# A Perceiver block on one core: filler steps as lists with kinds and lags, VectorE's parts held back, gating by tanh on ScalarE and GpSimd

## The chip, the core and the metric

The kernel runs on one core of a Trainium2 chip. The core's engines each work through their own queue in order: TensorE (PE; its weight loads are the row PEld), VectorE (DVE), ScalarE (ACT), GpSimd (POOL) and SyncE (SP, which here only issues transfers). The metric is the device time of one execution in microseconds; three executions of the kernel before gave 1245.61, 1246.41 and 1250.19 us.

## The reference

64 sequences of 64 rows of 256 numbers (`x`) pass through three residual stages; `ctx_1024` holds 256 context rows for each sequence. There are 16 heads of 16 numbers, everywhere in fp32.

```python
x = x + _L0_xattn_ref(_layernorm(x), ctx_1024, ctx_1024, Wq, bq, Wk, bk, Wv, bv, Wo, bo)   # 64 queries, 256 keys
x = x + _L0_attn_ref(_layernorm(x), w_qkv, b_qkv, w_out, b_out)                            # causal, 64 keys
x = x + _L0_ffn_ref(_layernorm(x), w_gate, w_up, w_down)
...
gate = jax.nn.silu(_bitlinear(x, w_gate)); up = _bitlinear(x, w_up)
return _bitlinear(gate * up, w_down)          # inner width 1024
```

`_bitlinear` quantises each row of its input to steps of its largest magnitude over 127 and the weights to -1, 0 and 1 times one scale. Silu is `silu(z) = z * sigmoid(z)`, which equals `(z/2) * (1 + tanh(z/2))`.

## The kernel before

The 64 sequences ("images") form 8 groups of 8. The main loop (L659 to L700) runs over images, and each image does its cross attention; the self attention of the group before and the feed-forward of the group before that are cut into steps that fill the gaps. The order of instructions on PE, ACT, DVE and POOL is the order in which the program issues them (`manual_schedule`, L645): nothing reorders them later. An instruction whose input is late therefore holds everything behind it on its engine.

Cross attention of image n, in the order of issue:

- `scores` (L260): TensorE writes all 16 heads' scores transposed into one PSUM tile `sc` of four banks. There is one such tile (`bufs=1`), so the next image's scores wait until this one's Exp has read it. VectorE then reduces it with a transposition to maxima `tm` (L275) and `m` (L279).
- `cross_av` (L318) of the image before: TensorE multiplies its probabilities `PT` by the values into `av`, and sums of them `PS` by ones; ScalarE takes one half of the rows (`keep`, L335).
- `project` (L632): one of four quarters of the next image pair's keys (L219, L232) or values (L239, L242).
- `fill()`: filler steps.
- `cross_keep` (L339) takes the other half of the rows on VectorE.
- `max_rows` (L284): TensorE transposes the maxima (`mtp`, L288), and a chain of six VectorE instructions (L290 to L297) turns them into bf16 rows `mr`.
- `cross_out` (L341): VectorE's reciprocal (L342) and multiplication (L344) give `yT_a`.
- `probabilities` (L301): TensorE subtracts the maxima by adding products of `mr` (L306); ScalarE takes Exp of `sc` into `PT` in two halves (L313); GpSimd adds the two key halves into `PS` (L315).
- `project` and `fill` again, and the next image's `scores`.

In an image there are five calls of one filler step each: one ahead of `max_rows`, one ahead of `probabilities`, one after it, two ahead of the next `scores`. The steps are two Python generators, `self_attention` (L347) and `ffn` (L497), and `fill` (L593) takes one step from each in turn until one is exhausted. What is left at the start of a group is run out by `drain` (L601). A list `later` takes a few VectorE parts (L433, L535) and is emptied ahead of the next step; other VectorE parts are issued inside their steps: the masking, maxima and sums of the self attention (L387, L390, L401), the residual additions (L252, L562), layer-norm statistics (L177), the row scales of the quantisation (L488 to L494). `prepare` (L609) does the next group's layer norm and queries, one part per image from image 1 of a group on, after the load of its `x` (L83).

The self attention works on 128-row tiles: scores `ssc` (L381), masking and maxima on VectorE, subtraction on GpSimd (L391), Exp on ScalarE (L395), sums on VectorE (L401), division on GpSimd (L403), transposition (L411), product `sav` (L426), output projection (L249).

The feed-forward takes its four row tiles one after the other. `gate_up` (L525) computes one half of the inner width: two products gate and up of 512 columns in PSUM (L529), Silu of gate on ScalarE into SBUF (L532), and on VectorE `up * unit * silu` into `h` (L538). Two calls make a row tile. Then come the row scale (L488 to L494), two roundings on ScalarE (L544, L548), transposition (L553, L555), the down product (L560) and the addition to `x` (L562); `out[g]` is stored from GpSimd's queue (L580).

Every product that is not `sc` uses one of four PSUM tiles `mm` (L69), taken in turn. After the last image, group 7's self attention runs with group 6's feed-forward, and then group 7's feed-forward alone.

Of the kernel before, what the change touches and what calls it, by code (L numbers as in the profile page):

```python
# [34 lines left out]
P = 128  # L36
D = 256
# [21 lines left out]
def tile_perceiver(ctx: ExitStack, tc: tile.TileContext, a: dict, out: bass.AP):  # L59
# [137 lines left out]
    def ln_apply(src, y, b, name):  # L197

        xn = act.tile([P, NI, D], F32, tag="xn", name=f"xn_{name}", bufs=3)
        for i in range(NI):  # L200
            nc.scalar.activation(xn[:, i, :], src[:, i, :], AF.Identity, bias=b[:, i:i + 1],
                                 scale=y[:, i:i + 1])
        return xn
# [40 lines left out]
    def add_projected(w, yT, xg, name, i0):  # L244

        pm = mm_tile(f"o_{name}_{i0}")
        for i in range(2):
            for kc in range(KC):
                nc.tensor.matmul(pm[:, i * D:(i + 1) * D],  # L249
                                 yT[:, kc, (i0 + i) * P:(i0 + i + 1) * P], w[:, kc, :],  # L250
                                 start=(kc == 0), stop=(kc == KC - 1))
        nc.vector.tensor_tensor(xg[:, i0:i0 + 2, :], pm.rearrange("p (i d) -> p i d", d=D),  # L252
                                xg[:, i0:i0 + 2, :], ALU.add)
# [30 lines left out]
    def max_rows(n, m3):  # L284
# [5 lines left out]
        nc.vector.tensor_reduce(x, pt[:, 0:P].rearrange("p (r i) -> p i r", i=32), AX.X, ALU.max,  # L290
                                negate=True)
        for k in range(2):
            t = small.tile([P, 32], BF16, tag="mt", name=f"mt_{n}_{k}")
            nc.vector.tensor_copy(t, x)
            nc.vector.scalar_tensor_tensor(x, t, term[:, k:k + 1], x, ALU.mult, ALU.add)
# [22 lines left out]
    def cross_av(n, pT, pS, v):  # L318
# [17 lines left out]
        return a4, t  # L336

    def cross_keep(a4, t):
        nc.vector.scalar_tensor_tensor(t, a4[:, :, 1, :], par[:, 1:2], t, ALU.mult, ALU.add)  # L339

    def cross_out(n, t, yT):  # L341
        nc.vector.reciprocal(t[:, KC:, :], t[:, KC:, :])  # L342
        b = n % G
        nc.vector.tensor_tensor(yT[:, :, b * T:(b + 1) * T], t[:, 0:KC, :], t[:, KC:, :], ALU.mult)  # L344


    def self_attention(g, xg, yTa):  # L347
        nm = f"s{g}"
        mv = moments(nm)
        for i0 in range(0, NI, 2):  # L350
            add_projected(wT["o"], yTa, xg, f"a{g}", i0)
            ln_stats(xg, nm, mv, (i0, i0 + 1))
            yield
        y, shift = ln_rstd(mv, nm)
        yield
        xn = ln_apply(xg, y, shift, nm)
        yield
        xnT = act.tile([P, KC, NT], F32, tag="xnT", name=f"xnT_{nm}")
        for kc in range(KC):
            transposed(xn, nm, xnT, kc)  # L360
        yield
        qm = act.tile([P, KC, G, 2, T], F32, tag="sqm", name=f"sqm_{g}", bufs=1)
        kT = act.tile([P, KC, NT], F32, tag="skT", name=f"skT_{g}", bufs=1)
        v = act.tile([P, NI, D], F32, tag="sv", name=f"sv_{g}", bufs=1)
        for hg in range(KC):
            queries(wqkv, bqm2, xnT, nm, qm, hg)
            yield
            keys(wqkv, D, bqkc[:, KC + hg:KC + hg + 1], xnT, nm, kT, hg)
            yield
        yT = act.tile([P, KC, NT], F32, tag="yT", name=f"yT_{nm}", bufs=3)  # L370
        s, pTs = {}, {}

        def scores(hg, j0):
# [3 lines left out]
            for b in range(G):  # L377
                for h in range(2):
                    for i in range(2):
                        r = slice(2 * E * (j0 + i), 2 * E * (j0 + i + 1))  # L380
                        nc.tensor.matmul(scs[i][h * T:(h + 1) * T, b * T:(b + 1) * T],  # L381
                                         qm[r, hg, b, h, :], kT[r, hg, b * T:(b + 1) * T],
                                         start=True, stop=True)
            for i in range(2):
                k = f"{nm}_{hg}_{j0 + i}"
                t = s[hg, j0 + i] = att.tile([P, G, T], F32, tag="s", name=f"s_{k}", bufs=4)
                nc.vector.tensor_tensor(t, scs[i].rearrange("p (b k) -> p b k", k=T),  # L387
                                        causal.unsqueeze(1).to_broadcast([P, G, T]), ALU.add)
                mx = small.tile([P, G], F32, tag="smax", name=f"smax_{k}")
                nc.vector.tensor_reduce(mx, t, AX.X, ALU.max)  # L390
                nc.gpsimd.tensor_tensor(t, t, mx.unsqueeze(2).to_broadcast([P, G, T]), ALU.subtract)  # L391
# [5 lines left out]
        def normalise(hg, j0):  # L397
            for j in (j0, j0 + 1):
                t = s[hg, j]
                tot = small.tile([P, G], F32, tag="stot", name=f"stot_{nm}_{hg}_{j}")  # L400
                nc.vector.reduce_sum(tot, t, axis=AX.X)  # L401
                nc.vector.reciprocal(tot, tot)  # L402
                nc.gpsimd.tensor_tensor(t, t, tot.unsqueeze(2).to_broadcast([P, G, T]), ALU.mult)  # L403
# [14 lines left out]
        def product(hg):  # L418

            av = [mm_tile(f"sav_{g}_{hg}_{bl}") for bl in range(2)]  # L420
            for bp in range(G // 2):
                for bl in range(2):
                    r = slice(bl * T, (bl + 1) * T)
                    for j in range(NJ):
                        d0 = hg * P + 2 * E * j
                        nc.tensor.matmul(av[bl][2 * E * j:2 * E * (j + 1), bp * P:(bp + 1) * P],  # L426
                                         v[r, bp, d0:d0 + 2 * E], pTs[hg, j][r, bp, :], start=True,
                                         stop=True)
            for bl in range(2):
# [3 lines left out]
                later.append(lambda bl=bl, a4=a4, t=t: keep(hg, bl, a4, t))  # L433

        def keep(hg, bl, a4, t):
            y4 = yT[:, hg, :].rearrange("p (bp bl q) -> p bp bl q", bl=2, q=T)
# [3 lines left out]
        scores(0, 0)  # L440
        yield
        values(wqkv, 2 * D, xnT, nm, v, 0)
        exps(0, 0)
        yield
        scores(0, 2)
        normalise(0, 0)
        yield
        values(wqkv, 2 * D, xnT, nm, v, 2)
        exps(0, 2)
        yield  # L450
        transpose(0, 0)
        normalise(0, 2)
        yield
        scores(1, 0)
        yield
        transpose(0, 2)
        exps(1, 0)
        yield
        scores(1, 2)
        normalise(1, 0)  # L460
        yield
        product(0)
        exps(1, 2)
        yield
        transpose(1, 0)
        normalise(1, 2)
        yield
        add_bias(xg, bo2_r, 0)
        yield
        transpose(1, 2)  # L470
        yield
        product(1)
        add_bias(xg, bo2_r, 2)
        yield
        mv = mvs[g] = moments(f"f{g}")
        for i0 in range(0, NI, 2):
            add_projected(wout, yT, xg, nm, i0)
            ln_stats(xg, f"f{g}", mv, (i0, i0 + 1))
            yield
# [17 lines left out]
    def ffn(g, xg):  # L497
        nm = f"f{g}"
        mv = mvs.pop(g)
        y, shift = ln_rstd(mv, nm)  # L500
        yield
        xn = ln_apply(xg, y, shift, nm)
        yield
        scale, unit = row_scale(xn, f"x{g}")
        u = small.tile([P, 2, NI], F32, tag="units", name=f"units_{g}", bufs=2)
        nc.vector.tensor_scalar(u[:, 0, :], unit, g_unit, None, ALU.mult)
        nc.vector.tensor_scalar(u[:, 1, :], unit, u_unit, None, ALU.mult)
        yield
        for i in range(NI):
            nc.vector.tensor_scalar(xn[:, i, :], xn[:, i, :], scale[:, i:i + 1], MAGIC, ALU.mult,  # L510
                                    ALU.add)
        q = act.tile([P, NI, D], BF16, tag="q", name=f"q_{nm}", bufs=1)
        nc.scalar.activation(q, xn, AF.Identity, bias=unmagic)
        yield
        pt = mm_tile(f"qtp_{nm}", BF16)
        for i in range(NI):
# [260 lines left out]
```

## Time and profile before

| what | us |
|---|---|
| median of the runs | 1246.41 |
| the profiled execution | 1248.42 |
| its span, first to last instruction | 1246.7 |
| DVE L275, maxima with transposition, each | 2.302 |
| ACT L313, Exp of half of `sc`, each | 1.020 |
| POOL L315, `PS`, each | 1.270 |
| POOL L391, subtraction, each | 1.043 |
| DVE L538, gating, each | 0.747 |
| ACT L532, Silu, each | 0.687 |
| ACT table loads ahead of L532, L313, L395 and L201: 27, 18, 8, 1, each | 1.283 |
| TensorE waiting at L306 for `mr`, in all | 110.3 |
| GpSimd waiting at L315 for `PT`, in all | 390.7 |

How to read it: a group row gives line, engine, operation, output and inputs with their shapes, the number of instances, then their busy time and mean duration in ns, then the idle time of the engine ahead of them with what ended it. The row of a window gives its length and the busy time of PE, PEld, DVE, ACT and POOL (with counts), the granted TensorE clock, the share of the DMA engines and GB/s. A timeline row gives start, duration, engine, line and instruction, and in brackets the engine's idle time before it and what ended it.

### The profile page before, as it was taken

What the parts mean: (1) busy time and instruction counts of PE and PEld (TensorE: products, weight loads), DVE (VectorE), ACT (ScalarE), POOL (GpSimd) and SP (SyncE); (2) the same over time, 40 slices, a digit from 0 to 9 for tenths busy, and PEclk for the clock granted to TensorE, in tenths of its full rate; (3) what the DMA queues carried; (4) which work ended last, traced back from release to release, by engine and by line L of the source; (5) the groups of instructions that cost most, each with busy time, mean ns of one, the idle gap of its engine ahead of it and who ended that gap; (6) DMA issues with size and microseconds to landing.
All of it is one profiled execution on the core that took longest, in us unless ns stands there. A gap on an engine that the chain in (4) does not pass through costs nothing. (4 is left out here: it accounts for less than half of the span.)

```text
span 1246.7 us, 25915 instructions
## 1 busy us (share of the span) xinstructions
PE 955.5 (77%) x11086; PEld 630.8 (51%) x11086; DVE 778.2 (62%) x1616; ACT 665.8 (53%) x934; POOL 412.2 (33%) x502
## 2 busy tenths in 40 slices
PE   6666688887787788787787787788886887676755
PEld 3444456564455545564455554555454654553532
DVE  1465667656667756576666765767575766775634
ACT  2233255436764386536774377544864467536635
POOL 1234335332235323334143422443134422341330
PEclk9878898988998898888998998988988888888868
DMA  6111000000001000010000100010000100000000
GB/s 197 52 51 52 18 18 19 18 19 17 18 19 36 18 34 1 19 52 18 18 18 2 52 18 18 18 52 18 18 2 18 35 18 1 2 18 1 1 18 17
DMA packets 10195, 32.44 MB, mean 26 GB/s; under 512 B 2400, under 2 KB 2784, under 8 KB 9696
## 3 DMA queue, kind: packets, MB, share of 16 engines
q1 hardware_dynamic: 7056, 26.22, 6.4%
q0 software_dynamic: 1152, 4.19, 0.8%
q8 instruction: 87, 1.43, 0.5%
q10 hardware_dynamic: 1872, 0.37, 0.2%
q14 instruction: 28, 0.23, 0.1%
HBM read 26.59 MB, written 4.19 MB: 25 GB/s over the span
## 5 line engine op out<-in xcount | busy, mean ns | idle before, releaser
L315 POOL TENSOR_TENSOR PS<-PT 128x512 f32<-128x512 f32 x128 | 159.9, 1270 | 390.7 <-ACT PT L313 390.7
L275 DVE TRANSPOSE_TENSOR_REDUCE tm<-sc 128x64 f32<-128x2048 f32 x64 | 147.3, 2302 | 96.1 <-PE sc L271 96.0
L313 ACT ACTIVATE PT<-sc 128x1024 f32<-128x1024 f32 x128 | 123.9, 1020 | 123.4 <-PE sc L306 123.2
L219 PE MATMUL k_a<-cT,wk 128*128 128x512 f32 x256 | 144.3, 694 | 6.8 <-DMA wk<-in_wk_dram 5.6
L239 PE MATMUL v_a<-wv,cT 128*128 128x256 f32 x512 | 144.6, 432 | 1.2 <-ACT sqm L227 1.2
L391 POOL TENSOR_TENSOR s_s<-s_s,smax_s 128x512 f32<-128x512 f32 x64 | 66.7, 1043 | 226.5 <-DVE smax_s L390 221.3
L538 DVE SCALAR_TENSOR_TENSOR h_f<-up_f,units,silu_f 128x512 f32<-128x512 f32 x64 | 47.8, 747 | 125.0 <-ACT silu_f L532 124.1
L239 PEld LDWEIGHTS v_a<-wv,cT 128*128 128x128 f32 x512 | 104.8, 214 | 32.7 <-issue 12.6
L306 PE MATMUL sc<-mr,ones 32*128 32x512 bf16 x256 | 31.1, 470 | 110.8 <-DVE mr L297 110.3
L335 ACT ACTIVATE keep<-av,par 128x256 f32<-128x256 f32 x64 | 30.3, 473 | 134.0 <-PE av L331 134.0
L219 PEld LDWEIGHTS k_a<-cT,wk 128*128 128x128 f32 x256 | 54.0, 223 | 60.5 <-issue 50.9
L232 ACT ACTIVATE kT<-k_a,bk_c 128x512 f32<-128x512 f32 x64 | 43.9, 688 | 72.2 <-PE k_a L219 72.1
L271 PE MATMUL sc<-qm,kT 32*128 32x128 f32 x2048 | 79.0, 292 | 1.5 <-ACT qm L227 0.9
L271 PEld LDWEIGHTS sc<-qm,kT 32*128 32x128 f32 x2048 | 66.3, 195 | 24.6 <-issue 14.0
L306 PEld LDWEIGHTS <-ones 32*128 32x128 bf16 x256 | 11.3, 93 | 132.8 <-issue 130.8
L326 PE MATMUL av<-PT,v 128*32 128x128 f32 x2048 | 74.7, 289 | 0.0
L387 DVE TENSOR_TENSOR s_s<-ssc,causal 128x512 f32<-128x512 f32 x64 | 43.9, 685 | 48.0 <-PE ssc L381 48.0
L403 POOL TENSOR_TENSOR s_s<-s_s,stot_s 128x512 f32<-128x512 f32 x64 | 65.4, 1043 | 5.7 <-DVE stot_s L402 3.0
L342 DVE RECIPROCAL keep<-keep 128x128 f32<-128x128 f32 x64 | 60.5, 945 | 0.0
L326 PEld LDWEIGHTS av<-PT,v 128*32 128x32 f32 x2048 | 55.6, 115 | 9.1 <-issue 1.2
L529 PEld LDWEIGHTS <-qT_f 128*128 128x128 bf16 x256 | 25.8, 104 | 63.3 <-issue 47.4
L560 PE MATMUL down_f<-wq_down,hqT_f 128*128 128x256 bf16 x256 | 41.8, 319 | 20.0 <-ACT hqT_f L555 20.0
(159 smaller groups left out, 1970.5 us busy)
## 6 DMA issues: line engine op xcount, KB each, us to landing
cT<-in_ctx_dram SPq DMA_DIRECT2D x32, 512.0 KB, 3.6
x<-in_x_dram SPq DMA_DIRECT2D x8, 512.0 KB, 3.6
out_dram<-x POOLq DMA_DIRECT2D x8, 512.0 KB, 3.2
wffn_gate<-in_wgate_dram SPq DMA_DIRECT2D x1, 1024.0 KB, 4.8
wffn_up<-in_wup_dram SPq DMA_DIRECT2D x1, 1024.0 KB, 4.9
wffn_down<-in_wdown_dram SPq DMA_DIRECT2D x1, 1024.0 KB, 4.8
wqkv<-in_wqkv_dram SPq DMA_DIRECT2D x1, 768.0 KB, 6.2
wk<-in_wk_dram SPq DMA_DIRECT2D x1, 256.0 KB, 4.3
```

Source lines behind the costliest of these rows:

```text
L219: nc.tensor.matmul(pm, w[:, kc, c0:c0 + P], src[:, kc, :], start=(kc == 0), stop=(kc == KC - 1))
L232: nc.scalar.activation(kT[:, hg, :], pm, AF.Identity, bias=bias)
L239: nc.tensor.matmul(pm[:, i * D:(i + 1) * D], src[:, kc, (i0 + i) * P:(i0 + i + 1) * P], w[:, kc, c0:c0 + D], start=(kc == 0), stop=(kc == ...
L271: nc.tensor.matmul(sc[:, j, c, hg, :], kT[r, hg, k0 + c * P:k0 + (c + 1) * P], qm[r, hg, b, :, :].rearrange("p h q -> p (h q)"), start=not ...
L275: nc.vector.tensor_reduce(tm.rearrange("p j c m -> p (j c m)"), sc.rearrange("p j c g (b i) -> p (j c g b) i", i=32), AX.X, ALU.max, apply ...
L313: nc.scalar.activation(pT[:, j:j + 2].rearrange("p j c g q -> p j (c g q)"), sc[:, j:j + 2].rearrange("p j c g q -> p j (c g q)"), AF.Exp)
L315: nc.gpsimd.tensor_tensor(pS[:, j:j + 2], pT[:, j:j + 2, 0], pT[:, j:j + 2, 1], ALU.add)
L326: nc.tensor.matmul(av[2 * E * j:2 * E * (j + 1), hg * P:(hg + 1) * P], v[:, (n % 2) * SC + c, d0:d0 + 2 * E], pT[:, j, c, hg, :], start=(c ...
L342: nc.vector.reciprocal(t[:, KC:, :], t[:, KC:, :])
L391: nc.gpsimd.tensor_tensor(t, t, mx.unsqueeze(2).to_broadcast([P, G, T]), ALU.subtract)
L403: nc.gpsimd.tensor_tensor(t, t, tot.unsqueeze(2).to_broadcast([P, G, T]), ALU.mult)
L538: nc.vector.scalar_tensor_tensor(h[i][:, 0, n0:n0 + 512], up, u[:, 1, i:i + 1], sl, ALU.mult, ALU.mult)
```

## The change

Every filler becomes a list of steps `(kind, lag, function)`. Kind "H" marks steps whose VectorE parts are long, "L" steps that ScalarE finishes, and "Z" steps that issue nothing on TensorE; a lag is the least number of places until the step may run. Almost all VectorE parts of steps go into `later` with a length in microseconds, and so does the cross attention's output part (`cross_out` now holds `cross_keep` too). `fill(kind)` runs at most one step per place beside "Z" steps, with preference for a kind. Of a feed-forward's list the last four steps stay behind (`LEFT`) for the next group's first images. Output projections are split into one step per row tile. The store follows the last step of its list, `x` is loaded and `prepare` begun one image later, and `xn` has two buffers instead of three.

```diff
-        nc.vector.tensor_reduce(x, pt[:, 0:P].rearrange("p (r i) -> p i r", i=32), AX.X, ALU.max,
-                                negate=True)
         for k in range(2):
             t = small.tile([P, 32], BF16, tag="mt", name=f"mt_{n}_{k}")
-            nc.vector.tensor_copy(t, x)
+            if not k:
+                for o in (x, t):
+                    nc.vector.tensor_reduce(o, pt[:, 0:P].rearrange("p (r i) -> p i r", i=32), AX.X,
+                                            ALU.max, negate=True)
+            else:
+                nc.vector.tensor_copy(t, x)
...
+        later.append((1.4, lambda: cross_out(n, a4, t, yT)))
+    def cross_out(n, a4, t, yT):
         nc.vector.scalar_tensor_tensor(t, a4[:, :, 1, :], par[:, 1:2], t, ALU.mult, ALU.add)
         nc.vector.reciprocal(t[:, KC:, :], t[:, KC:, :])
-        nc.vector.tensor_tensor(yT[:, :, b * T:(b + 1) * T], t[:, 0:KC, :], t[:, KC:, :], ALU.mult)
+        nc.gpsimd.tensor_tensor(yT[:, :, b * T:(b + 1) * T], t[:, 0:KC, :], t[:, KC:, :], ALU.mult)
...
+        return [
+            *(step("H", 1, (add_cross, i)) for i in range(NI)), step("Z", 1, (root,)),
+            step("Z", 2, (norm,)), step("L", 1, (turn, 0)), step("L", 1, (turn, 1)),
+            step("L", 1, (query, 0)),
+            step("L", 1, (key, 0)), step("L", 1, (query, 1)), step("L", 1, (key, 1)),
+            step("H", 1, (scores, 0, 0)), step("L", 1, (value, 0)), step("H", 1, (scores, 0, 2)),
+            step("L", 1, (value, 2), (exps, 0, 0)), step("Z", 1, (normalise, 0, 0), (exps, 0, 2)),
+            step("L", 2, (transpose, 0, 0), (normalise, 0, 2)), step("H", 1, (scores, 1, 0)),
+            step("L", 1, (transpose, 0, 2)), step("H", 1, (scores, 1, 2)),
+            step("H", 1, (product, 0), (exps, 1, 0)), step("Z", 1, (normalise, 1, 0), (exps, 1, 2)),
+            step("L", 2, (transpose, 1, 0), (normalise, 1, 2)), step("Z", 1, (add_bias, xg, bo2_r, 0)),
+            step("L", 1, (transpose, 1, 2)), step("H", 1, (product, 1), (add_bias, xg, bo2_r, 2)),
+            *(step("H", 1, (add_self, i)) for i in range(NI))]
...
-            sl = act.tile([P, 512], F32, tag="silu", name=f"silu_{nm}_{i}_{n0}")
-            nc.scalar.activation(sl, gate, AF.Silu, scale=u[:, 0, i:i + 1])
...
-            nc.vector.scalar_tensor_tensor(h[i][:, 0, n0:n0 + 512], up, u[:, 1, i:i + 1], sl, ALU.mult,
-                                           ALU.mult)
+            a = h[i][:, 0, n0:n0 + 512]
+            t, u = (act.tile([P, 512], F32, tag=k, name=f"{k}_{nm}_{i}_{n0}") for k in ("tanh", "up"))
+            nc.scalar.activation(t, gate, AF.Tanh, scale=d["u"][:, 0, i:i + 1])
+            nc.scalar.activation(a, gate, AF.Copy, scale=d["u"][:, 0, i:i + 1])
+            nc.scalar.activation(u, up, AF.Copy, scale=d["u"][:, 1, i:i + 1])
+            nc.gpsimd.tensor_tensor(a, a, u, ALU.mult)
+            nc.gpsimd.tensor_tensor(t, t, a, ALU.mult)
+            nc.gpsimd.tensor_tensor(a, a, t, ALU.add)
...
+        def first_half(i):
+            if i >= 2 and i - 2 < NI:
+                round_hidden(i - 2)
             if i < NI:
                 gate_up(i, 0)
+            if i >= 3:
+                down(i - 3)
+        def second_half(i):
             if i < NI:
                 gate_up(i, 512)
             if 0 < i <= NI:
+                later.append((2.1, lambda: scale_hidden(i - 1)))
+            if i >= 2:
+                turn_hidden(i - 2)
...
+    def flush(us=1e9):
+        while later and us > 0:
+            t, f = later.pop(0)
+            us -= t
+            f()
...
+    def fill(kind):
+        place[0] += 1
+        able = [k for k in range(2) if len(streams[k]) > LEFT * k and ready[k] <= place[0]]
+        for k in list(able):
+            if streams[k][0][0] == "Z":
+                run(k)
+                if not streams[k] or ready[k] > place[0] or streams[k][0][0] == "Z":
+                    able.remove(k)
+        if able:
+            run(max(able, key=lambda k: (streams[k][0][0] == kind,
+                                         len(streams[k]) / count[k] - 0.4 * k)))
...
         if done is not None:
-            kept = cross_av(n - 1, *done, vs[(n - 1) // 2])
-        next(ahead, None)
+            cross_av(n - 1, *done, vs[(n - 1) // 2], yTs[(n - 1) // G])
         if bp + 1 < B // 2:
             project(bp + 1, 2 * (n % 2))
-        fill()
-        if kept is not None:
-            cross_keep(*kept)
+        flush(1.5)
+        fill("L")
         mr = max_rows(n, m3)
-        if kept is not None:
-            cross_out(n - 1, kept[1], yTs[(n - 1) // G])
+        flush()
...
-        fill()
+        for _ in range(2):
+            fill("H")
+            flush()
         done = probabilities(n, sc, mr)
-        fill()
         if bp + 1 < B // 2:
             project(bp + 1, 2 * (n % 2) + 1)
-        fill(2)
+        next(ahead, None)
+        fill("H")
+        flush()
+        fill("L")
...
-        if b == 0 and g + 1 < NG:
+        if b == 1 and g + 1 < NG:
+            if g > 2:
+                while len(streams[1]) > count[1]:
+                    run(1)
...
-    fill(60)
-    streams[:] = [ffn(NG - 1, xs[NG - 1]), iter(())]
-    fill(60)
+    while streams[0]:
+        fill("L")
+        flush()
+    begin(1, ffn(NG - 1, xs[NG - 1]))
+    finish(1)
```

In the changed kernel the gating's three GpSimd lines are L551 to L553, its ScalarE lines L548 to L550, the maxima L274, the chain L293 to L299, the products with `mr` L308, the Exp L315, `PS` L317, the self attention's masking L405, the held-back addition L576.

## The prediction

> **What bounds the kernel now.** I read the engine shares first, then the starts of the row for line 275 in time order, then the busy table of one group of eight images and of the two closing stretches, then one slow image line by line, then the group rows.
>
> ```profile
> PE 955.5 (77%) x11086; PEld 630.8 (51%) x11086; DVE 778.2 (62%) x1616; ACT 665.8 (53%) x934; POOL 412.2 (33%) x502
> ```
>
> No engine is full; TensorE is nearest. Line 275 runs once per image. Its starts give the pace: images 32 to 39 start 21.4, 14.2, 14.9, 17.1, 26.2, 15.4, 23.4, 10.9 us apart, 143.4 us in all, and groups 3 to 6 (images 24 to 55) repeat this to 0.1 us. Group 0 takes 124.5, group 1 114.8, group 2 136.8, the seven steps of group 7 124.9, and 146.9 us follow the last start (1099.8). The stretches (columns: PE, PEld, DVE, ACT, POOL busy, granted clock, DMA):
>
> ```profile
> 544.90:688.30 143.40, 115.03 (x1392) 76.34 (x1392) 94.81 (x200) 84.50 (x118) 49.38 (x62) 0.90 0.07 24
> 1099.80:1200.50 100.70, 72.64 (x813) 49.10 (x813) 60.14 (x137) 52.97 (x77) 33.81 (x44) 0.80 0.03 12
> 1200.50:1246.70 46.20, 19.82 (x104) 10.60 (x104) 18.38 (x47) 23.31 (x27) 3.15 (x9) 0.75 0.03 12
> ```
>
> So in a full group TensorE idles 28.4 us of 143.4. Where, the image of 26.2 us shows (timeline):
>
> ```profile
> 618.22 0.69 DVE L387 TENSOR_TENSOR s_s<-ssc,causal 128x512 f32<-128x512 f32 x1 [2.50 <-PE ssc L381]
> 618.94 0.69 DVE L390 TENSOR_REDUCE smax_s<-s_s 128x8 f32<-128x512 f32 x1
> 619.55 0.68 DVE L387 TENSOR_TENSOR s_s<-ssc,causal 128x512 f32<-128x512 f32 x1
> 621.03 1.04 POOL L391 TENSOR_TENSOR s_s<-s_s,smax_s 128x512 f32<-128x512 f32 x1 [0.27 <-DVE smax_s L390]
> 621.57 0.54 DVE L294 CAST mt<-mx 128x32 bf16<-128x32 f32 x1
> 623.41 0.61 PE L306 MATMUL sc<-mr,ones 32*128 32x512 bf16 x4 [2.43 <-DVE mr L297]
> 623.95 3.78 PE L239 MATMUL v_s<-wqkv,xnT_s 128*128 128x256 f32 x8
> 624.10 1.28 ACT L313 ACT_TABLE_LOAD   x1 [2.73 <-issue]
> 625.39 1.94 ACT L313 ACTIVATE PT<-sc 128x1024 f32<-128x1024 f32 x2
> ```
>
> VectorE's self-attention parts (L387, L390) stand in its queue ahead of the maxima chain (L290 to L297), whose last product `mr` TensorE awaits; then a table load delays the Exp which alone frees the score tile. The chain scores, maxima, `mr`, L306, Exp is the period's frame; mr ends 110.3 us of TensorE's waits in the whole run, the largest cause. The rows that price the change:
>
> ```profile
> L315 POOL TENSOR_TENSOR PS<-PT 128x512 f32<-128x512 f32 x128 | 159.9, 1270 | 390.7 <-ACT PT L313 390.7
> L538 DVE SCALAR_TENSOR_TENSOR h_f<-up_f,units,silu_f 128x512 f32<-128x512 f32 x64 | 47.8, 747 | 125.0 <-ACT silu_f L532 124.1 <-PE up_f L529 1.0
> L532 ACT ACTIVATE silu_f<-gate_f,units 128x512 f32<-128x512 f32 x64 | 44.0, 687 | 13.5 <-PE gate_f L529 13.2
> L532 ACT ACT_TABLE_LOAD x27 | 34.6, 1283 | 0.5
> ```
>
> [...] The built program holds 1 load after, 54 before. [...] the L294 cast above took 0.54 us beside a GpSimd operation that ended at 622.07, elsewhere 0.18. [...] v_s above took 3.78 us after a 2.43 us gap, v_a of the same shape 1.99 us in the image before.
>
> **The change, part by part.**
>
> *Gating.* Removed: 64 Silu (44.0 us of ACT), 53 table loads (68.0), 64 L538 (47.8 of DVE). Added: 3 x 64 activations of 512 columns from PSUM at 0.687 (the Silu and kT rows) = 131.9 on ACT, net +19.9; 3 x 64 GpSimd operations with two full inputs at 1.27 (L315, L256; L391's 1.04 has a broadcast input and is my low end) = 243.8. One gate-and-up call thus costs 2.06 us of ACT and 3.81 us of GpSimd. tanh and up have two buffers each, so ACT's next call but one waits for GpSimd; behind it on ACT stands, at times, the Exp.
>
> *Other moves.* L344's 64 multiplications (20.9 us) go to GpSimd, at 0.40 each by size from 1.27: 25.6; they feed only the next group's projection, so cover is ample. A cast becomes a second reduction (0.273 to 0.285): nothing. L252 halves: 64 x 0.425 (L141's row) for 32 x 0.687, +5.2 on DVE. DVE nets -63 us, GpSimd goes from 412 to about 682. The reciprocal (0.94) and the keep (0.47) move ahead of the maxima chain; beside them TensorE does av, a projection and an L step (1.7 + 2.0 + about 1.2), more than line 275 and 279 plus these (2.3 + 0.4 + 1.4), so hidden; without filler steps (group 0) it costs about 0.2 us an image. The x load moves one image later and behind a store (3.6 and 3.2 us to landing) on SP's queue, ahead of the next cT load; both have an image of 12 us or more. xn with two buffers instead of three: sets are used within two images, nothing. The store on GpSimd's queue waits for the held-back addition at L576, with the next layer norm's small operations behind it; an image's length covers that.
>
> *Steps.* A group has 40 non-"Z" steps for 40 places, so every image gets five; two are placed between the maxima's transposition and L306, where the chain needs 2.0 us of VectorE and two steps give TensorE 2 to 4 us. From the built order and the row means I summed TensorE's work by image: 40 12.2, 41 11.7, 42 16.8, 43 14.6, 44 14.6, 45 14.5, 46 17.8, 47 14.8 us. Held-back parts keep line 275 prompt.
>
> *What is late next.* Six of a group's eight gate-and-up calls fall in images 45 and 46. Walking 44 to 46 by the queues with these durations: 44 takes 15.0 us. In 45 ACT must do four Exp of the self attention (2.5) and a call (2.06) ahead of the cross attention's Exp, which starts 4 us after L306 is done; TensorE then lacks PSUM tiles; 19.2 us. In 46 ACT has quantising (2.4), two calls (4.1) and copies ahead: 23 us. That is 57.2 against 46.9 of work. For 47 I take 15.5; 40 to 43, little above their work, 57.5. Group: 130 us. [...] I leave 130, with 120 (no waits, 117 of work) and 138 as ends.
>
> *Sum over the profiled execution (1246.7 span, 1248.4 itself, 2.0 above the median).* Group 0: 0. Group 1 (self attention alone; work spread over more images): -8, from 114.8 to 107. Group 2: from 136.8 to 129, -8. Groups 3 to 6: 4 x -13.4 = -53.6. Group 7: seven steps, from 124.9 to 112, -13. Tail: the last self attention now shares with six gate calls in a row (the tail asks for kind L first): 6 x 3.81 = 23 us on GpSimd ahead of its second score pair, of which earlier queries and keys and less left over from before win back about 15: +8 (0 to +16). Last feed-forward alone: before 1200.5 to 1242.0; after, prelude 13.6, GpSimd paces the eight calls (first 2.1, then 30.4), then row scale, rounding, transposition, product about 8: 54 against 41.5, +12. Total -8 -8 -54 -13 +20 = -63: about 1185 against 1248.4, 1183 against the median. I say 1180[...].
>
> **Rivals.** *TensorE-bound* (chance 0.18): buffers absorb ACT's and GpSimd's bursts, a group takes 120. -9 -17 -94 -20 -3 = -143: about 1105. For: GpSimd's 81 us and ACT's 87 per group are below 120; against: they crowd into two images. *Waits only move* (0.12): a group takes 138[...]: -5 +2 -22 -5 +24: about 1240. *GpSimd holds TensorE* (0.10), the losing side: in-order GpSimd has the PS sums behind gate calls, PS is needed by av, so TensorE stops once a call. From the forecast, 63 us over 64 calls is 1.0 us: if each call holds TensorE 1.0 us longer than I reckon, the gain is gone[...]. Against it: before, POOL waits 43.7 us a group for PT alone, so it has slack in most images. The change does do what it says: order and load count are in the built program.
>
> **Numbers.** Forecast 0.60 at 1180, own range 1145 to 1220 (group 124 to 136, tail +8 to +28). Range 1120 to 1242 leaves out about half of the first rival and the last. About 0.5% (6 us) is what a measurement of this kernel can tell from no change: faster 0.85, within 0.05 (part of the second rival), slower 0.10.
>
> **What would show it.** Right: one table load; starts of line 274 repeating near 130 us a group, images 45 and 46 the longest; Exp there waiting behind ACT's own work; POOL near 680 us busy; waits of L308 for mr well below 110 us; the last feed-forward near 54 us. Wrong: equal images near 15 us (first rival), or av or ACT waiting on GpSimd by tens of microseconds in every group (last one).

## The result, and the profile after

The changed kernel takes 1254.32 us (median of 20 runs, 1240.36 to 1264.32); the kernel before, on the same chip, 1248.24 (20 runs). Four of the 20, the profiled one (span 1259.8) among them, are slow, over 1.5% above the fastest; without them the median is 1253.0, which the differences below use, and the ratio is 1.0029, 95% interval 1.0009 to 1.005. That is no difference that counts. The forecast was 1180. Single microseconds of after's profile may be that execution's own; for the main readings other kernels' profiles are set beside it.

The engine shares of after, the page's first line:

```profile
PE 968.8 (77%) x11086; PEld 630.9 (50%) x11086; DVE 737.9 (59%) x1520; ACT 671.1 (53%) x1009; POOL 684.8 (54%) x758
```

GpSimd (POOL) is at 684.8 us, where the prediction reckoned 682, and there is one table load. VectorE (DVE) lost 40 us and not the 63 reckoned (the last section says where most of the difference lies). TensorE (PE) needs 13 us more in this execution for the same 11,086 instructions. The waits view (who waits for whom: us in total, times, longest), the line for `mr` before, then after:

```profile
PE sc L306 <- DVE mr L297: 110.3, 45, 5.0
```

```profile
PE stp L432 <- POOL s_s L424: 54.4, 24, 6.8
PE sc L308 <- DVE mr L299: 41.0, 23, 4.7
ACT h_f L560 <- DVE qscale_hf L497: 27.2, 6, 6.3
PE stp L432 <- DVE x L576: 21.5, 5, 5.4
```

The wait that the change aimed at (`mr`, L306 before, L308 after) fell from 110.3 to 41.0 us. In its place stands a new one, 54.4 us: the transpositions of the self attention's probabilities (L432) wait for GpSimd's product with the reciprocal sums (L424). In x1_silu, a changed kernel told below, the wait for `mr` is 36.9 us.

The starts of L274 (L275 before) in time order give each stretch. The fourth column is an experiment that is told below, in which no part is held back. All are spans of one profiled execution, us:

| stretch | before | forecast | after | nothing held back |
|---|---|---|---|---|
| ahead of the first image | 25.5 | 25.5 | 25.9 | 25.4 |
| group 0 | 124.5 | 124.5 | 129.0 | 128.9 |
| group 1 | 114.7 | 107 | 125.2 | 112.7 |
| group 2 | 136.8 | 129 | 138.4 | 136.1 |
| groups 3 to 6 | 573.5 | 520 | 545.5 | 514.7 |
| group 7, seven steps | 124.8 | 112 | 122.6 | 114.2 |
| after the last start | 146.9 | 167 | 173.0 | 169.4 |
| span | 1246.7 | 1185 | 1259.8 | 1201.4 |

So the closing stretch lost what was forecast, and a little more; what is missing is the groups' gain. Group 0 has no steps to place, and its length scatters with the same code (128.9 us with nothing held back, 125.7 and 124.4 in x17_silu_all_now and x18_all_bias02, which hold nothing back either), so nothing is read from it. Busy time by stretch (columns as before: PE, PEld, DVE, ACT, POOL, clock, DMA), first for group 1 before, then in after for group 1, for group 4 and for the closing stretch up to and from the last feed-forward's normalisation:

```profile
150.02:264.70 114.68, 98.72 (x1287) 66.21 (x1285) 74.29 (x152) 53.39 (x84) 46.69 (x54) 0.93 0.07 22
```

```profile
154.94:280.24 125.30, 101.31 (x1288) 67.46 (x1287) 71.59 (x149) 53.14 (x84) 49.94 (x60) 0.90 0.06 18
555.73:691.79 136.06, 113.61 (x1389) 74.64 (x1388) 91.12 (x187) 82.96 (x127) 83.78 (x93) 0.92 0.08 25
1086.77:1202.90 116.13, 76.08 (x749) 49.67 (x742) 55.65 (x138) 60.09 (x86) 65.58 (x76) 0.74 0.03 10
1202.90:1259.80 56.90, 23.68 (x104) 11.63 (x104) 14.21 (x39) 31.80 (x42) 30.80 (x26) 0.59 0.02 10
```

In group 4 TensorE still idles 22.4 us of 136.1 (28.4 of 143.4 before). In group 1, where there is no feed-forward and so no gating, it idles 24.0 us, 16.0 before (x1_silu, whose instructions are the same up to there, has 24.0 too). The timeline of after shows why, in the fifth image of group 1:

```profile
219.12 0.43 DVE L299 TENSOR_TENSOR mr<-mx,mask 128x256 bf16<-128x256 f32 x1
219.46 0.68 DVE L422 TENSOR_REDUCE stot_s<-s_s 128x8 f32<-128x512 f32 x1
220.53 2.04 POOL L424 TENSOR_TENSOR s_s<-s_s,stot_s 128x512 f32<-128x512 f32 x2 [3.16 <-DVE stot_s L423]
221.62 0.80 PE L432 MATMUL stp<-ident,s_s 128*128 128x128 f32 x4 [2.76 <-POOL s_s L424]
...
223.67 0.61 PE L308 MATMUL sc<-mr,ones 32*128 32x512 bf16 x4
224.21 3.78 PE L220 MATMUL k_a<-cT,wk 128*128 128x512 f32 x4
```

`mr` is done at 219.5, prompt as intended. But the sums (L422), held back, begin only then. GpSimd's product follows at 220.5, and the transposition, which stands ahead of L308 in TensorE's queue, waits 2.76 us for it. L308 comes at 223.7, 4.1 us after its own input was ready. The next product (`k_a`, 1.98 us elsewhere) takes 3.78, at a granted clock of 0.50. This wait and one of 5.04 us in the next image come to 7.8 us, as much as the group's 8.0 more of idle time.

Late sums are 23.7 of the 54.4 us, in seven waits of this kind. In eight others, 26.4 us in all, the sums are done early and the held-back product stands on GpSimd behind a gate call, as in the sixth image of group 4:

```profile
642.47 0.20 DVE L423 RECIPROCAL stot_s<-stot_s 128x8 f32<-128x8 f32 x1
...
643.10 1.27 POOL L551 TENSOR_TENSOR h_f<-h_f,up_f 128x512 f32<-128x512 f32 x1 [0.34 <-ACT up_f L550]
...
645.80 1.26 POOL L553 TENSOR_TENSOR h_f<-h_f,tanh_f 128x512 f32<-128x512 f32 x1
...
647.03 2.04 POOL L424 TENSOR_TENSOR s_s<-s_s,stot_s 128x512 f32<-128x512 f32 x2
...
648.12 0.66 PE L432 MATMUL stp<-ident,s_s 128*128 128x128 f32 x4 [2.16 <-POOL s_s L424]
```

There the transposition holds up the next image's scores (650.17 on TensorE).

### The profile page after: what moved, and what is told of

It is laid out like the page before. It is cut to its first block, busy times and chain, and to the rows that moved or that the text cites. A ratio compares the mean times of both kernels' runs of the same rounds, so it can differ in the third digit from the quotient of the medians.

```text
span 1259.8 us, 26085 instructions
## 1 busy us (share of the span) xinstructions
PE 968.8 (77%) x11086; PEld 630.9 (50%) x11086; DVE 737.9 (59%) x1520; ACT 671.1 (53%) x1009; POOL 684.8 (54%) x758
## 4 chain that ended last, share of the span: by engine, by line
PE 39%; DVE 29%; POOL 14%; ACT 12%; issue 5%; DMA 1%; POOLq 0%; ACTq 0%; DVEq 0%
PE k_a L220 7%; DVE tm L274 7%; PE sc L270 5%; PE v_a L240 5%; DVE keep L342 3%; POOL tanh_f L552 3%; PE av L328 3%; POOL h_f L551 2%; DVE mx L297 2%; POOL s_s L424 2%; PE stp L432 2%; PE q_a L220 2%; POOL h_f L553 2%; PE q_s L220 2%; PE ssc L396 2%
## 5 line engine op out<-in xcount | busy, mean ns | idle before, releaser
L274 DVE TRANSPOSE_TENSOR_REDUCE tm<-sc 128x64 f32<-128x2048 f32 x64 | 147.9, 2311 | 225.4 <-PE sc L270 225.4
L317 POOL TENSOR_TENSOR PS<-PT 128x512 f32<-128x512 f32 x128 | 160.2, 1272 | 144.6 <-ACT PT L315 144.6
L315 ACT ACTIVATE PT<-sc 128x1024 f32<-128x1024 f32 x128 | 124.0, 1024 | 69.7 <-PE sc L308 63.2
L220 PE MATMUL k_a<-cT,wk 128*128 128x512 f32 x256 | 152.9, 728 | 9.6 <-DMA wk<-in_wk_dram 5.6
L344 POOL TENSOR_TENSOR yT_a<-keep 128x128 f32<-128x128 f32 x64 | 29.0, 454 | 180.4 <-DVE keep L342 180.0
L432 PE MATMUL stp<-ident,s_s 128*128 128x128 f32 x256 | 51.6, 350 | 75.9 <-POOL s_s L424 54.4
L337 ACT ACTIVATE keep<-av,par 128x256 f32<-128x256 f32 x64 | 30.3, 473 | 146.8 <-PE av L333 146.8
L551 POOL TENSOR_TENSOR h_f<-h_f,up_f 128x512 f32<-128x512 f32 x64 | 81.2, 1269 | 49.9 <-ACT up_f L550 49.9
L270 PE MATMUL sc<-qm,kT 32*128 32x128 f32 x2048 | 87.2, 313 | 8.3 <-ACT PT L315 5.5
L270 PEld LDWEIGHTS sc<-qm,kT 32*128 32x128 f32 x2048 | 73.5, 213 | 33.1 <-issue 12.4
L552 POOL TENSOR_TENSOR tanh_f<-tanh_f,h_f 128x512 f32<-128x512 f32 x64 | 83.8, 1310 | 5.0
L553 POOL TENSOR_TENSOR h_f<-h_f,tanh_f 128x512 f32<-128x512 f32 x64 | 81.4, 1271 | 5.0
L432 PEld LDWEIGHTS stp<-ident,s_s 128*128 128x128 f32 x256 | 36.6, 176 | 91.3 <-POOL s_s L424 65.2
L424 POOL TENSOR_TENSOR s_s<-s_s,stot_s 128x512 f32<-128x512 f32 x64 | 65.3, 1041 | 23.6 <-DVE stot_s L423 23.6
L405 DVE TENSOR_TENSOR s_s<-ssc,causal 128x512 f32<-128x512 f32 x64 | 43.5, 680 | 55.4 <-PE ssc L396 47.8
L243 ACT COPY v<-v_a 128x512 f32<-128x512 f32 x64 | 37.6, 589 | 56.9 <-PE v_a L240 56.7
```

The lines of the kernel that those rows point to most:

```text
L220: nc.tensor.matmul(pm, w[:, kc, c0:c0 + P], src[:, kc, :], start=(kc == 0), stop=(kc == KC - 1))
L270: nc.tensor.matmul(sc[:, j, c, hg, :], kT[r, hg, k0 + c * P:k0 + (c + 1) * P], qm[r, hg, b, :, :].rearrange("p h q -> p (h q)"), start=not ...
L274: nc.vector.tensor_reduce(tm.rearrange("p j c m -> p (j c m)"), sc.rearrange("p j c g (b i) -> p (j c g b) i", i=32), AX.X, ALU.max, apply ...
L315: nc.scalar.activation(pT[:, j:j + 2].rearrange("p j c g q -> p j (c g q)"), sc[:, j:j + 2].rearrange("p j c g q -> p j (c g q)"), AF.Exp)
L317: nc.gpsimd.tensor_tensor(pS[:, j:j + 2], pT[:, j:j + 2, 0], pT[:, j:j + 2, 1], ALU.add)
L432: nc.tensor.transpose(pt[:, bp * P:(bp + 1) * P], t[:, 2 * bp:2 * bp + 2, :].rearrange("p b k -> p (b k)"), ident)
```

## The experiments

Two suspects were named first: the gating (ScalarE's and GpSimd's longer way for each call), and the held-back sums as in the lines above. Times are medians; each ratio is to the kernel before on the same chip, with its 95% interval, and all sixteen but x3_tanh_dve lie over 1% from it. The table collects all sixteen (G1: group 1; G3-6: groups 3 to 6; tail: after the last start; us of the profiled span).

| kernel | time | ratio | G1 | G3-6 | tail |
|---|---|---|---|---|---|
| x1_silu | 1227.2 | 0.9851 (0.9826 to 0.9877) | 125.3 | 549.1 | 146.8 |
| x2_before_tanh | 1301.1 | 1.0434 (1.0404 to 1.0465) | 114.7 | 587.1 | 176.7 |
| x3_tanh_dve | 1250.4 | 1.0031 (1.0012 to 1.0051) | 122.0 | 561.2 | 154.4 |
| x4_sums_now | 1225.9 | 0.9851 (0.9816 to 0.9886) | 117.2 | 529.1 | 169.5 |
| x5_silu_sums | 1212.6 | 0.9731 (0.9703 to 0.976) | 118.2 | 535.0 | 150.0 |
| x6_tail_silu | 1206.6 | 0.9678 (0.965 to 0.9705) | 117.2 | 530.1 | 149.8 |
| x7_tail_h | 1229.6 | 0.985 (0.9821 to 0.9878) | 119.4 | 528.8 | 170.6 |
| x9_down_now | 1226.3 | 0.9838 (0.9803 to 0.9873) | 119.3 | 527.9 | 172.4 |
| x10_lag | 1212.5 | 0.9713 (0.9693 to 0.9733) | 114.7 | 528.0 | 170.2 |
| x12_all_now | 1203.1 | 0.9633 (0.9615 to 0.9652) | 112.7 | 514.7 | 169.4 |
| x11_even | 1199.8 | 0.9609 (0.959 to 0.9629) | 117.2 | 518.5 | 160.6 |
| x14_bias02 | 1197.9 | 0.9604 (0.958 to 0.9627) | 117.2 | 520.3 | 160.8 |
| x15_masked_now | 1224.8 | 0.9822 (0.9793 to 0.985) | 115.8 | 526.8 | 169.6 |
| x16_scale_now | 1211.9 | 0.9718 (0.9687 to 0.9749) | 119.3 | 516.3 | 169.5 |
| x17_silu_all_now | 1177.5 | 0.9445 (0.9417 to 0.9473) | 112.6 | 514.4 | 146.9 |
| x18_all_bias02 | 1185.6 | 0.9502 (0.9474 to 0.9529) | 112.7 | 514.4 | 160.4 |

### Gating and sums, each by itself

x1_silu: the changed kernel with the gating of before.

```diff
-            nc.scalar.activation(t, gate, AF.Tanh, scale=d["u"][:, 0, i:i + 1])
...
-            nc.gpsimd.tensor_tensor(a, a, t, ALU.add)
+            nc.scalar.activation(sl, gate, AF.Silu, scale=d["u"][:, 0, i:i + 1])
+            later.append((0.75, lambda: nc.vector.scalar_tensor_tensor(
+                a, up, d["u"][:, 1, i:i + 1], sl, ALU.mult, ALU.mult)))
```

> The changed kernel with the gating of the kernel before: Silu on ScalarE and one VectorE product, held back like the other VectorE parts; its order has 64 table loads of 1.28 us, and GpSimd is freed of 244 us. Theory A (the gating by GpSimd eats what the lists gain): about 1225 us, since the loads give back part. Theory B (the held-back sums of the self attention stall TensorE at the transpositions in every group, gating or not): 1255 to 1275 us, the loads coming on top.

It takes 1227.2, 26 us less than after. Groups 1 and 2, and 3 to 6 together, are as in after to within 4 us, the table loads that are back (32 ahead of Silu and 23 ahead of the cross attention's Exp, 1.283 us each) notwithstanding; the tail is back at 146.8. So what gating by tanh costs, 26 us of the tail, lies where no cross attention runs beside it. The waits behind gate calls are gone, and the transpositions' waits for GpSimd's product are 27.9 us in place of 54.4. But at the same transpositions TensorE now waits 20.3 us for Silu and 9.8 for VectorE's product, so the groups are no shorter.

x2_before_tanh: the kernel before with the new gating (and two `xn` buffers in place of three, to make room).

> The kernel before with only the gating changed to tanh on ScalarE and three GpSimd products (and two xn buffers, which the new tiles need); one table load. Theory A: slower than before, 1265 to 1290 us, since each row scale now waits for up to 7.6 us of GpSimd in the old order. Theory B: the gating is no loss by itself, the missing 53 loads (68 us of ScalarE) give 1225 to 1245 us.

1301.1: 30 us more in the tail, and 3.4 more in each full group. In the old order the gating gains nothing in any stretch with a feed-forward (the third `xn` buffer's part in this was not tried).

x3_tanh_dve: tanh kept, with two VectorE products in place of GpSimd's three operations.

```diff
-            nc.gpsimd.tensor_tensor(a, a, u, ALU.mult)
...
+            nc.vector.scalar_tensor_tensor(t, t, 1.0, gate, ALU.add, ALU.mult)
+            nc.vector.scalar_tensor_tensor(a, up, d["u"][:, 1, i:i + 1], t, ALU.mult, ALU.mult)
```

> The changed kernel with tanh on ScalarE but the gate and up products taken from PSUM by two VectorE instructions (about 0.75 us each, 96 us in all), no GpSimd gating, one table load. Theory A: 1205 to 1220 us. Theory B: 1240 to 1255 us, the transpositions still waiting for the sums.

1250.4: the tail gains 19 us and groups 3 to 6 lose 16, as VectorE gets the work: GpSimd is the right place for it in the groups and the wrong one in the tail.

x4_sums_now: the sums emitted where their step is.

```diff
-                later.append((0.85, lambda j=j: divided(hg, j)))
+                divided(hg, j)
```

> The changed kernel with one edit: the self attention's sums and reciprocals (L422, L423) are issued in their step and no longer held back behind the maxima. Theory A: within 5 us of the changed kernel, 1250 to 1258. Theory B: the waits of the transpositions L432 for GpSimd's division (54 us in the changed kernel's run) mostly go, 1225 to 1238 us.

1225.9: 27 us less than after; the spans have 8 less in group 1 and 16 in groups 3 to 6. TensorE's waits for GpSimd's product fall from 54.4 to 15.7 us (of those behind a gate call none is left in groups 3 to 7), and those for `mr` rise from 41.0 to 49.4.

x10_lag leaves the sums held back and asks for the transpositions later (lags 2, 1, 2, 1 become 3, 2, 4, 2).

> The changed kernel with the normalising sums still held back behind the maxima, but the transpositions that read their product asked for one or two places later (lags 2, 1, 2, 1 become 3, 2, 4, 2). If the 28 us come from TensorE standing at transpositions ahead of line 308 while VectorE's held-back sums and GpSimd's product are still to come, they come back here without touching the sums: 1226 to 1235, and the waits of stp for s_s on TensorE's matmul queue fall from 54 to below 20 us. If instead the late sums cost by delaying what follows on VectorE and GpSimd, the later transpositions change nothing: 1250 to 1260.

1212.5, and that wait at 14.7 us, with everything still held back: what costs is TensorE standing at a transposition too early, not the late sums as such. It gained more than expected, 40 us for 19 to 28, and not all of it is that wait's. The lags also move the gate calls to other images, ScalarE's waits for the row scale fall from 27.2 to 2.5 us, and TensorE's for L576 from 21.5 to nothing.

### What else is held back

x12_all_now holds nothing back (tanh gating kept):

```diff
-    later = []
+    class Now(list):
+        def append(self, p):
+            p[1]()
+    later = Now()
```

> The changed kernel with nothing held back at all: every VectorE part is emitted where its step is (tanh gating kept). If holding back behind the maxima is worth what the waits of line 308 for mr lost (110 to 41 us), those come back: 1226 + 30 to + 60 = 1256 to 1286. If the steps' spacing by lags did the work and holding back is only a wash, 1220 to 1235.

It was expected to lose and takes 1203.1, 50 us less than after. The waits view of this kernel, and the stretches of its groups 1 and 4:

```profile
PE sc L308 <- DVE mr L299: 57.9, 34, 4.7
PE stp L432 <- POOL s_s L424: 18.3, 17, 4.3
```

```profile
154.37:267.06 112.69, 96.67 (x1286) 65.82 (x1284) 72.59 (x149) 53.05 (x84) 49.78 (x60) 0.94 0.07 20
529.14:658.98 129.84, 110.46 (x1383) 74.74 (x1388) 94.06 (x187) 83.08 (x127) 83.20 (x93) 0.93 0.08 26
```

Holding back saves 17 us of waits for `mr` (57.9 against 41.0) and costs, with these lags, 50 us of time; x10 shows that 40 of them can be had back without giving it up. The rest of the fall from 110.3 comes without it. Against after, group 4 loses 3.1 us of TensorE's idle time and 3.1 of its busy time, the latter at a higher granted clock (0.93 for 0.92); group 1 loses 8.0 and 4.6. Over groups 3 to 6 it is 11 of idle and 20 of busy time (0.95 for 0.92): more of the gain lies in TensorE's busy time than in its gaps.

Three runs take single parts on top of the sums. x9_down_now emits the feed-forward's last addition (L576) at once, x15_masked_now the masking and maxima of the scores, x16_scale_now the row scales.

> Sums at once, and the feed-forward's last addition also emitted at once, in place of being held back. TensorE waits 17.9 us in all for that addition at the transpositions (its PSUM tile is freed late). If that wait is real: 1226 - 8 to -15 = 1211 to 1218. If the wait only covers another one (the tile of the next in turn), 1224 to 1228; if it costs the maxima chain (0.7 us each on VectorE's queue, 28 of them) 1228 to 1240.

1226.3, and the wait of the transpositions for that addition unmoved at 17.4 us: a miss for the idea. In the queue the row scale stays ahead of it.

> The changed kernel with two of the held-back parts at once: the normalising sums (as in the run that has those alone, 1226) and the masking and maxima of the self attention's scores (1.4 us each, 64 of them). Emitting everything at once gave 1203. If masking is what makes up the other 23 us (scores' PSUM tiles and GpSimd's subtraction come late): 1203 to 1210, group 1, which has no feed-forward, near 113. If the row scales do: 1222 to 1228, or more, as the masking then stands ahead of the maxima again: up to 1240.

1224.8: nothing measurable.

```diff
-            later.append((2.3, scale_rows))
+            scale_rows()
...
-                later.append((2.1, lambda: scale_hidden(i - 1)))
+                scale_hidden(i - 1)
```

> Sums at once, and the feed-forward's row scales at once (2.1 us for each of four tiles of 128 rows and 2.3 for a group's entry) in place of held back; masking and the additions stay held back. If the row scales are what makes up the other 23 us, since ScalarE stands at the quantisation with tanh and Exp behind it: 1203 to 1212, image 46 of a group near 22 us in place of 26.8, group 1 unchanged at 117. If masking does: 1222 to 1228.

1211.9, 14 us less than with the sums alone; the seventh image of a full group (46 in group 5) falls from 26.9 to 22.0 us as expected. The timeline of x4_sums_now shows what went away, in the same image one group earlier:

```profile
643.71 1.42 DVE L299 TENSOR_TENSOR mr<-mx,mask 128x256 bf16<-128x256 f32 x1
645.05 1.21 DVE L493 TENSOR_REDUCE amax_hf<-h_f 128x1 f32<-128x1024 f32 x1
646.87 1.24 ACT L560 ACTIVATE h_f<-h_f,magic,qscale_hf 128x1024 f32<-128x1024 f32 x1 [3.63 <-DVE qscale_hf L497]
...
648.15 0.63 PE L432 MATMUL stp<-ident,s_s 128*128 128x128 f32 x4 [3.38 <-DVE x L576]
649.20 0.67 ACT L548 ACTIVATE tanh_f<-gate_f,units 128x512 f32<-128x512 f32 x1
650.50 3.78 PE L220 MATMUL k_a<-cT,wk 128*128 128x512 f32 x4 [1.39 <-ACT h_f L549]
```

The row scale (from L493) waits for `mr`; ScalarE stands 3.63 us at the quantisation that needs it (L560), with the next call's tanh behind it; the addition that would free a PSUM tile (L576) comes after the row scale on VectorE, so TensorE stands 3.38 us. ScalarE's waits for the scale fall from 23.9 to 5.1 us in x16. Groups 3 to 6 in x4_sums_now, then in x16_scale_now:

```profile
408.79:937.92 529.13, 453.21 (x5533) 297.96 (x5532) 368.50 (x744) 330.73 (x503) 334.09 (x372) 0.92 0.08 25
410.91:927.18 516.27, 436.60 (x5511) 291.59 (x5533) 369.30 (x745) 329.60 (x503) 333.93 (x372) 0.95 0.08 26
```

TensorE's idle time does not fall (75.9 us, then 79.7); its busy time does, by 16.6 us, at a granted clock of 0.95 for 0.92. Of the 23 us between sums alone and nothing held back, 14 are the row scales'; the other 9, about 7 of them in group 1 (119.3 to 112.7), come with the remaining parts together (additions, moments, keep, masking) and aren't assigned to one.

### The tail

x7_tail_h (on top of x4_sums_now) asks for kind H first in the closing loop, in place of L.

> Sums at once, and in the closing loop the self attention's steps of kind H are asked for first, in place of kind L. If the tail loses its time by six gate calls in a row ahead of the last self attention's scores, as the prediction reckoned, the tail falls from 170 by 5 to 15 us: 1211 to 1221. If the loss is the last feed-forward alone (GpSimd's three operations per call and the longer way to the row scale), nothing moves: 1224 to 1228, or a few us longer as fewer of the gate calls of group 6 are done early.

1229.6, tail 170.6. The last of the scores now end at 57.6 us of the tail in place of 85.9, and the last feed-forward begins at 113.5 all the same, 112.3 without the edit. The order isn't what costs.

x6_tail_silu (sums at once) gives the feed-forwards of groups 6 and 7 alone the old gating, x5_silu_sums all of them.

```diff
+            if g >= NG - 2:
+                nc.scalar.activation(sl, gate, AF.Silu, scale=d["u"][:, 0, i:i + 1])
...
+                return
```

> The changed kernel with both suspected costs undone: Silu and VectorE's held-back product in place of tanh and GpSimd (64 table loads return), and the sums of the self attention's normalising emitted at once. If the two costs are separate places (26 us in the closing stretch, 28 us in the groups), they add: 1254 - 27 - 28 = 1199 us, tail near 145, groups 3 to 6 near 133. If they share the same waits (GpSimd's queue behind gate calls is what makes the late sums late), one undone leaves little of the other: 1215 to 1227.

> Sums at once, and Silu with VectorE's product only for the feed-forwards of groups 6 and 7, the two that run in the closing stretch; the six others keep tanh and GpSimd. If tanh gating costs only where no cross attention covers GpSimd's three operations, this takes back the whole tail: 1226 - 23 = 1203 us, tail near 147, and beats the one with Silu everywhere by what 48 table loads fewer are worth (0 to 5 us). If gating by GpSimd also costs in the groups, it lies 5 us or more above the kernel with Silu everywhere.

1212.6 and 1206.6, both tails at 150, 20 below x4_sums_now's: the places don't fully add for x5 (14 more than the sum of both gains), and tanh within the groups is worth 6 us over Silu. The timeline of after in the last feed-forward shows what the tail pays:

```profile
1217.52 1.26 POOL L553 TENSOR_TENSOR h_f<-h_f,tanh_f 128x512 f32<-128x512 f32 x1
1218.74 1.26 POOL L551 TENSOR_TENSOR h_f<-h_f,up_f 128x512 f32<-128x512 f32 x1
1218.82 0.69 ACT L548 ACTIVATE tanh_f<-gate_f,units 128x512 f32<-128x512 f32 x1 [2.33 <-POOL h_f L553]
1220.08 1.27 POOL L552 TENSOR_TENSOR tanh_f<-tanh_f,h_f 128x512 f32<-128x512 f32 x1
1221.42 1.26 POOL L553 TENSOR_TENSOR h_f<-h_f,tanh_f 128x512 f32<-128x512 f32 x1
1222.64 1.27 POOL L551 TENSOR_TENSOR h_f<-h_f,up_f 128x512 f32<-128x512 f32 x1
```

A call each 3.9 us (L551 to L551), GpSimd without a gap, ScalarE waiting for it with the tanh buffer.

### The gains put together

x11_even and x14_bias02 start from x6_tail_silu and set the feed-forward's handicap in the choice of steps (`- 0.4 * k`) to 0 and 0.2. x17_silu_all_now is x6_tail_silu with nothing held back, x18_all_bias02 the same at handicap 0.2.

> The kernel with sums at once and Silu in the closing stretch, and the feed-forward's handicap of 0.4 in the choice of steps set to 0: the gate calls start at image 42 of a group and lie 1, 2, 2, 3 over images 42 to 45, where they lay 1, 2, 3, 2 over 43 to 46. If bunched calls set the long image 46 (26 us) and TensorE's 19 us of idle per group, a group falls by 4 to 8 us: 1207 - 20 to - 45 = 1162 to 1187. If the same waits appear wherever they fall: 1200 to 1212. As the self attention's last steps now run in a row at the group's end, it can also lose: up to 1225.

> As the run before with the handicap at 0.2: gate calls 1, 2, 2, 3 over images 43 to 46, the self attention's last steps less crowded. Bunching theory: between 1180 and 1200; waits that only move: 1200 to 1212.

> Nothing held back, and Silu for the feed-forwards of groups 6 and 7 only. If the tail's 20 us and the cost of holding back are separate places: 1203 - 20 = 1183 us, tail near 148 to 150. If not: 1190 to 1203.

> As the run before, with the feed-forward's handicap 0.2. If the two gains (9 us for spreading with the sums at once, 23 us for holding back nothing) add: 1183 - 9 = 1174 us. If both came from the same crowd at images 45 and 46: 1180 to 1188.

1199.8 and 1197.9: 7 and 9 us gained, short of the 20 to 45 hoped for from the first; groups 3 to 6 gain 10 to 12, the tail gives 11 back. x17 takes 1177.5, the best, 5.6% below before (5.3 to 5.8): the tail's cost and that of holding back are separate places and add. x18 takes 1185.6: with nothing held back the spreading gains nothing in the groups (514.4 in both), which fits crowded gate calls being late for the held-back parts and not by themselves.

## Why the prediction was wrong

The sum missed by 75 us of span: group 0 4.5, group 1 18.2, group 2 9.4, groups 3 to 6 25.5, group 7 10.6, tail 6.0, start 0.4. About 9 of the 75 are the profiled execution's own, by which it (1261.6) lies above the median of 1253.0.

*The step that failed* is in "Steps": "two steps give TensorE 2 to 4 us" between the maxima's transposition and L306, and "Held-back parts keep line 275 prompt." The second half held; no price was set on who waits for the held-back parts. One of the two steps can be the transposition whose input is itself held back until after `mr`. It then covers nothing and stands ahead of L308; or its product, issued late, comes behind a gate call on GpSimd (54.4 us in all, 15.7 with the sums in their step). The row scales do the same to ScalarE (27.2 us). With nothing held back 50 of the missing 73 us of the median return, and the sums by stretch come near: groups 3 to 6 514.7 for 520, group 7 114.2 for 112, tail 169.4 for 167. In the group this is in part luck: images 40 to 43 take 62.5 us where 57.5 were reckoned, 44 to 47 take 66.8 for 72.7.

*Groups 1 and 2* were also mis-sized: -8 each was expected from more even images, and without any holding back they show -2.0 and -0.7. In group 1 TensorE works 96.7 of 112.7 us, so there was little to take. Group 2 stays at 136 to 142 us in most of the kernels; x10's longer lags bring it to 131.5, near the 129 reckoned. Why was not tried.

*Gating.* Right in size: one table load; GpSimd 1269, 1310 and 1271 ns for the three operations (1270 reckoned), a call each 3.9 us for 3.81. ScalarE waits 13.5 us in all for GpSimd with a tanh buffer. The group lines of after:

```profile
L552 POOL TENSOR_TENSOR tanh_f<-tanh_f,h_f 128x512 f32<-128x512 f32 x64 | 83.8, 1310 | 5.0
L548 ACT ACTIVATE tanh_f<-gate_f,units 128x512 f32<-128x512 f32 x64 | 43.6, 682 | 21.4 <-POOL h_f L553 13.5 <-PE gate_f L542 7.8
L344 POOL TENSOR_TENSOR yT_a<-keep 128x128 f32<-128x128 f32 x64 | 29.0, 454 | 180.4 <-DVE keep L342 180.0
```

*Tail.* +26 for +20, +22.5 with nothing held back. The last feed-forward alone, from its normalisation to its last addition, went from 38.1 to 52.1 us, +14 for +12; the part ahead of it +12.4 for +8, and +8.4 with nothing held back. The reason given for the latter (six calls in a row ahead of the scores) fell with x7: another order ends no sooner.

*What is late next*: right for 46 and 45, not for 44. In after's group 5 image 46 is the longest (24.5 us), then 44 and 45 (20.2 and 19.4); in 45 and 46 Exp does start behind ScalarE's own work, 2.1 to 2.2 us after L308 where the walk had 4. The walk had 15.0, 19.2 and 23 for 44 to 46; with nothing held back they take 15.1, 16.1 and 22.0.

*Rivals.* "Waits only move" came nearest: groups at 136 for its 138, an estimate, by the queues; what VectorE's longer operations (last section) add to that was not tried. "GpSimd holds TensorE" named the right pair of engines and was right in part: gate calls stand ahead of what TensorE needs for 26.4 us, though at the product with the sums and not at `PS`. As the whole cause it is refuted by x1_silu, which has no gating on GpSimd and groups as long. "TensorE-bound" is refuted by 22 us of idle time a group.

## What to carry to other kernels

Before an operation is held back behind a critical chain, follow its result: if its consumer stands ahead of the chain's end in another in-order queue, the chain waits for it after all, by way of that engine (L308 came 4.1 us after `mr`). Either the operation goes back to its step (x4, x16) or the consumer moves later (x10); the two together were not tried. A filler step covers a wait only if its own inputs are ready when the wait begins; the transposition of group 1 waited 2.76 us itself. An engine that is slower for an operation can be free where other work sets the pace, as GpSimd was in the groups with operations of 1.27 to 1.31 us, three a call, for VectorE's one of 0.75 (x6 takes 6 us less than x5); where a part of the program runs alone, try the faster engine there (20 us of the tail in x6), even at the price of table loads of 1.283 us each.

## What had not been expected of the hardware

After gaps, TensorE's products were often slow. Of the records that hold a whole `k_a` or `v_a` product (2.0 us elsewhere), 26 of 124 took over 3 us in after, 15 of 124 with nothing held back and 18 of 124 before. In after 25 of the 26 had a gap of over 2 us within the 8 us ahead of them; of the 98 others, 22 had. In the lines above it is 3.78 us each, at a granted clock of 0.50, soon after gaps of 2.76 and 3.38 us, with short transpositions and L308 between gap and product; against 1.98 us that is about half the rate. The largest case is x16 against x4: one gap of about 3.38 us in each full group goes, the time that TensorE spends at half the clock in groups 3 to 6 falls from 81.9 to 47.8 us, and with no less idle time they are 13 us shorter. What lowers the clock is not shown.

VectorE's short operations took longer in the groups with GpSimd's gating. The group lines of after:

```profile
L297 DVE SCALAR_TENSOR_TENSOR mx<-mt,term,mx 128x32 f32<-128x32 bf16 x128 | 50.6, 396 | 4.6
L296 DVE CAST mt<-mx 128x32 bf16<-128x32 f32 x64 | 24.1, 376 | 2.2
```

L297 took 264 ns before and takes 278 in x1_silu, which has no gating on GpSimd. In groups 3 to 6 it is 434 ns in after, 251 before and 252 in x1_silu; in group 1, without gating, 272. In all it went from 33.7 to 50.6 us, 17 of the 23 us that VectorE's relief fell short of. With nothing held back L297 takes 458 ns and L299 551 in place of 445, and the kernel is 50 us faster: such stretching did not stop the gain, and what it costs was not tried.
